# Layer 0's row steps behind its edge checks, constants and checks moved, later turns of the supports: one change to a four-layer graph kernel

## The chip, the cores and the metric

The kernel runs on one NeuronCore of a Trainium2 chip. The time is the device time of one execution in microseconds (us); lower is better. PE is the matrix engine, DVE the vector engine, ACT the scalar engine, POOL is GpSimd, and SP is the engine whose queue issues the large loads.

## The reference, cut to what matters

4096 nodes with 64 features each pass through four layers over the same dense 4096 x 4096 adjacency matrix of zeros and ones. Each layer ends with `x = layernorm(x + layer(x, adj))`.

```python
# layer 0: mean over the neighbours
deg = clip(sum(adj, axis=1) + 1.0, 1.0)
h   = (adj @ X + X) / deg
out = relu(concat([X, h]) @ W + b);  out = out / max(norm(out), 1e-12)
# layers 1 and 3: hyperbolic attention
adj_att   = sigmoid(left[:, None] + right[None, :] + b_att) * adj
x_local   = logmap(x[:, None, :], x[None, :, :])        # a vector for each pair of nodes
support_t = einsum('ij,ijd->id', adj_att, x_local);  out = proj(expmap(x, support_t))
# layer 2: at most 100 last neighbours, weighted by powers of 0.5
support = x @ weight
rank = cumsum(adj != 0, axis=1);  out = (mask * 0.5**(k - pos)) @ support + bias
```

## The kernel before, in words

**Tiling.** The nodes are 32 blocks of 128 rows (`NB = 32`, `P = 128`). The targets are taken in four groups of 1024 columns, in the order `GROUPS` = s 3, 2, 1, 0. For each group a layer walks `g` from 15 down to 0; each step loads two blocks of sources against the group's 1024 targets, a tile `edges` of 128 x 2 x 1024 numbers, 1 MB (`load`, line 708, on SP's queue). The matrix doesn't stay on the chip: each of the four layers reads its 64 tiles again. The pool of these tiles has 6 buffers, so load n+6 is issued when every reader of load n is done, and SP issues strictly in order.

**The check.** The fast path holds only where all edges are 0 or 1, so each of the 64 tiles is checked once in the whole kernel, by one DVE instruction over the tile (`check`, line 871). `checked_later(s, g)` names the tiles that are checked not in layer 0 but in layer 2 (`load_2`): g in 0, 1, 2, 3, 5, 7, 9, 11, half of each group. So in layer 0 a tile has two readers, the eight matmuls of line 1571 and, for g = 15, 14, 13, 12, 10, 8, 6, 4, the check.

**Row work and its turns.** What is done to a group's rows once their sums are there (in layer 0 `end_0`, then `norm_rows` and `prepare`, which make the operands of layer 1) is written as generators. `later` puts a generator in a queue, `tick` runs one step of each queue whose time has come, and `yield n` says how many ticks the next step waits. Layer 0 calls `tick(4)` after each load's matmuls, layer 2 `tick(1)` after each block. PE and ACT keep the order in which the program is written down (`manual_schedule(engines=FIXED)`); the instructions of DVE are put in order by a scheduler, so a row step may stand before or behind a check. `mark` records the last instruction of the main work on each engine (in `pairs_last`), and where `anchored[0]` is true, gives each row instruction of PE, ACT or DVE an order behind it. In layer 0 `anchored[0]` is false; from the second group of layers 1 and 3 on it is true.

**Layer 0 (line 1571).** Each load feeds eight matmuls of 512 columns. In the first group the loads are also interleaved with four pieces of x, split into bf16 parts by `parts_of` (lines 1472 to 1476). After the load g = 13 of the first group `constants()` (lines 1480 to 1494) is written down as one piece: a matmul that spreads the small vectors over the partitions (line 1481), its copy `given_b` (line 1482), eight small matmuls with the attention weights (line 855), and some fifty DVE instructions on one or two columns (`curved`, `att_columns`). Then follows `linear` for the group's own part (lines 1379 to 1390 and 1505). When a group's sums are complete, ACT copies them (lines 1596, 1604) and `end_0` is queued; its steps run during the next group. Its DVE chain goes from `deg` (1525) over `z` (1527 to 1548), `n_m`, `n_v` (924 to 938), `x`, `cx`, `y` (944 to 968) to `ys` (987) and `tt` (1006); PE then turns `ys` (1025).

**Layer 2.** The first pass (`wide_pass`) takes the groups 3 and 2 together, two loads a step; `narrow_pass` takes the others. Lines 1756 (running counts), 1763 (powers on ACT) and 1768 (weighted sums) are its work. In its early steps it also makes the last two blocks' `supports`: ACT rounds x to f16 (`x_hl`, 1403), GpSimd subtracts (1404), PE turns the two (1409) after a `yield 2`, ACT copies `x_t` (1412), PE multiplies (1419), ACT and DVE write `halves` (1425, 1426).

Of the kernel before, what the change touches and what calls it, by code (L numbers as in the profile page):

```python
# [21 lines left out]
D = 64  # L22
# [39 lines left out]
def gnn_stack_kernel(  # L62
# [509 lines left out]
    def stream(fits):  # L572

        with ExitStack() as st:
# [57 lines left out]
            def later(steps, second=False, wait=0):  # L632
                queues[int(second)].append([steps, place[1] + wait])

            def in_turn(tag, *parts):
                for part in parts:
                    yield from (part or ())
                done.add(tag)
# [5 lines left out]
            def need(tag):  # L644
                while tag not in done:
                    assert any(queues), tag
                    tick(1)
# [38 lines left out]
            def spare_ends():  # L686
                while held:
                    tick(1)
                spare.clear()
# [21 lines left out]

            def checked_later(s, g):

                return g in (0, 1, 2, 3, 5, 7, 9, 11)

            def grp(name, bufs=None):
                kw = {"bufs": bufs} if bufs else {}
# [129 lines left out]
                nc.scalar.dma_start(t, src[:, :, None, :].to_broadcast([1, 2, 2, D]))  # L847
                return t

            def att_columns(rows_of, name):  # L850


                t = aux.tile([P, 2], F32, name="aux")
                for u in range(2):
                    nc.tensor.matmul(
                        t[:, u : u + 1], rows_of[:, u].rearrange("p k d -> p (k d)"),
                        one_row[:, :1], start=True, stop=True,
                    )
                w = row.tile([P, 2], F32, name="att_w")
                V.tensor_copy(w, t)  # L860
                parts = keep.tile([P, 7], BF16, name=name)
                for k in range(3):
                    of = parts[:, k : k + 4 : 3]
                    V.tensor_copy(of, w)
                    V.tensor_sub(w, w, of)
                V.memset(parts[:, 6:], 1.0)
                return parts
# [530 lines left out]
            def supports(s):  # L1398


                xg = x_of(2)[:, blocks(s), :]
                hl = row.tile([P, WB, 2 * D], F16, name="x_hl")
                nc.scalar.copy(hl[:, :, :D], xg)
                nc.gpsimd.tensor_sub(hl[:, :, D:], xg, hl[:, :, :D])
                yield 2
                yield from free()
                t = take(F16, P, WW)
                for k in range(WB):
                    nc.tensor.transpose(t[:, k * P : (k + 1) * P], hl[:, k, :], ident16)
                yield near()  # L1410
                xt = row.tile([P, W], F32, name="x_t").bitcast(F16)
                nc.scalar.copy(xt, t)
                held.pop()
                yield near()
                yield from free()
                t = take(F32, P, WB, D)
                for k in range(WB):
                    for part in range(2):
                        nc.tensor.matmul(
                            t[:, k, :], xt[:, k * P : (k + 1) * P], w2_hl[:, part],  # L1420
                            start=part == 0, stop=part == 1,
                        )
                yield near()
                at = blocks(s)
                nc.scalar.copy(halves[:, at, :D], t)
                V.tensor_sub(halves[:, at, D:], t, halves[:, at, :D])
                held.pop()
                yield 1
# [25 lines left out]
            with ExitStack() as lp:  # L1454
# [23 lines left out]
                def constants():  # L1478

                    t = aux.tile([P, 2 * D + 3], F32, name="aux")  # L1480
                    nc.tensor.matmul(t, one_row, given, start=True, stop=True)
                    V.tensor_copy(given_b, t)
                    V.tensor_mul(c1, r_sb, r_sb)
                    V.reciprocal(c1, c1)
                    V.memset(c3, 1.0)
                    V.tensor_copy(ident16, ident)
                    V.memset(sum_w[:, D:], 0.0)
                    V.tensor_copy(sum_w[D:, :D], w0_sb[D:, :])
                    V.memset(count_w, 0.0)
                    V.memset(count_w[D:, D:], 1.0)  # L1490
                    V.tensor_copy(count_w[:D, :D], sum_w[:D, :D])
                    return (
                        curved(c1, "k1", 1e-15**0.5), curved(c3, "k3", 1e-15),
                        att_columns(att_rows1, "att1"), att_columns(att_rows3, "att3"),
                    )

                V.memset(third[:, :, D : D + 1], 1.0)
                parts_of(GROUPS[0])
# [8 lines left out]
                def end_0(s, tops):  # L1507
# [44 lines left out]
                        1, s, att1, batt1_sb, curve1, 1e-15, good[:, 0], 70  # L1552
                    )

                with tc.manual_schedule(engines=FIXED):
                    for s in GROUPS:
                        sums = [ps.tile([P, W], F32, name="acc") for _ in range(2)]
                        counts = [ps.tile([P, W], F32, name="acc") for _ in range(2)]
                        parts = ((first, sums, P), (third, counts, D + 1))
                        for g in reversed(range(NB // 2)):  # L1560
                            a, edge = load(s, g)
                            if s == GROUPS[0] and 2 * g % WB == WB - 2 and g > WB // 2:
                                parts_of(2 * g // WB - 1)
                            if not checked_later(s, g):
                                check(s, g, a, own.tile([P, 2, WW], BF16, name="junk"))
                            for k in (1, 0):
                                j = 2 * g + k
                                for lhs, accs, m in parts:
                                    for h in range(2):
                                        at = k * WW + h * W  # L1570
                                        nc.tensor.matmul(  # L1571
                                            accs[h][:m], lhs[:, j, :], edge[:, at : at + W],
                                            start=j == BLOCKS[0], stop=j == BLOCKS[-1],
                                        )
                            if g == s * WB // 2 + 1:

                                for lhs, accs, m in parts:
                                    for h in range(2):
                                        for k in range(SB):
                                            nc.tensor.matmul(  # L1580
                                                accs[h][:m, k * P : (k + 1) * P],
                                                lhs[:, s * WB + h * SB + k, :], ident_b,
                                                start=False, stop=False,
                                            )
                            if s == GROUPS[0] and g == NB // 2 - 3:
                                curve1, curve3, att1, att3 = constants()
                                nc.scalar.dma_start(w2_sb, w2)
                                nc.scalar.dma_start(w2_twice[:D], w2)
                                nc.scalar.dma_start(w2_twice[D:], w2)
                                later(in_turn((0, s), linear(0, s, w0_sb[:D, :], own_part)))  # L1590
                            tick(4)
                        need((0, s))
                        tops = []
                        for h in range(2):
                            top = row.tile([P, W], F32, name="sums", bufs=2)
                            nc.scalar.copy(top, sums[h])
                            low = (
                                row.tile([P, WB, D + 1], F32, name="u_1").rearrange(
                                    "p k f -> p (k f)"
                                )[: D + 1, :W]  # L1600
                                if h
                                else grp("w_att").rearrange("p k f -> p (k f)")[: D + 1]
                            )
                            nc.scalar.copy(low, counts[h][: D + 1])
                            tops.append((top, low))
                        later(end_0(s, tops))
                        if s == GROUPS[-1]:
                            need((0, s, "rows"))
                        if s > 0:
                            own_of = linear(0, s - 1, w0_sb[:D, :], own_part)  # L1610
                            later(in_turn((0, s - 1), own_of))

                spare_ends()


            place[0] = 1
# [286 lines left out]
```

## Time and profile before

| what | value |
|---|---|
| runs | 1061.79, 1062.61, 1067.7 us, median 1062.61 us |
| the profiled execution | 1063.81 us, of which its span, first to last instruction, is 1062.1 us |
| granted PE clock, mean | 0.975 of full |
| loads | 256 of 1 MB, four times 64 |

The stages, read from where the lines start and end:

| layer | from, to (us) |
|---|---|
| 0, groups 3, 2, 1, 0 (ACT starts to copy the sums) | 0, 54.2, 96.3, 139.7, 182.1 |
| 1 | 183 to 510 |
| 2, wide pass, then the narrow passes | 510 to 612, 612 to 720 |
| 3 and the end | 720 to 1062 |

How to read the profile: a row of the timeline has start and length in us, the engine, the line, the operation with its tiles, how many were merged, and in brackets how long the engine had been idle and what let it go. A row of the windows gives, for a stretch, its length, each engine's busy time with the number of instructions, the granted PE clock, the busy share of the DMA engines and what they moved in GB/s. A row of the waits gives in total how long an engine, or with a "q" its queue, waited for a group, how often, and the longest.

### The profile page before, as it was taken

To read this page: it belongs to the slowest core of one execution; us is meant where nothing else is said; L and a number is where in the kernel's file an instruction comes from. 1 tells how busy PE (TensorE), PEld (TensorE's weight loads), DVE (VectorE), ACT (ScalarE), POOL (GpSimd) and SP (SyncE) were. 2 spreads that over 40 slices of the span, in tenths; PEclk is the share of its full clock that TensorE was granted. 3 is DMA by queue.
4 is the path that set the end of the run, shared out by engine and by line. 5 is a ranking of instruction groups with operands and counts; after the bars stand their busy time and mean duration, and the time that the engine had idled before them with its cause. 6 is when DMAs were issued, how large, how long until landed. Compare 5 with 4: busy or idle time off the path is not lost.

```text
span 1062.1 us, 13509 instructions
## 1 busy us (share of the span) xinstructions
PE 981.6 (92%) x4760; PEld 401.9 (38%) x4845; DVE 900.2 (85%) x1383; ACT 753.1 (71%) x876; POOL 339.0 (32%) x695
## 2 busy tenths in 40 slices
PE   5998998889999999999999999999899999999991
PEld 2454554333333333333333344543333333333330
DVE  7577877788999999999475579858899999999996
ACT  0013122779989888898667688897898888888870
POOL 0011212480155365365210020104401562573660
PEclk8899999899999999999999999999999999999996
DMA  9999999755665666567589999996465765665600
GB/s 357 359 418 368 394 390 387 300 180 176 238 208 207 220 238 207 189 238 238 204 300 336 371 366 304 327 333 233 143 218 194 243 232 204 242 207 203 234 1 23
DMA packets 38580, 271.62 MB, mean 256 GB/s; under 512 B 4710, under 2 KB 4710, under 8 KB 5734
## 3 DMA queue, kind: packets, MB, share of 16 engines
q1 hardware_dynamic: 37728, 270.03, 69.6%
q8 instruction: 40, 0.66, 0.2%
q10 hardware_dynamic: 774, 0.63, 0.2%
q14 instruction: 38, 0.31, 0.1%
HBM read 269.58 MB, written 1.05 MB: 255 GB/s over the span
## 4 chain that ended last, share of the span: by engine, by line
PE 62%; DVE 21%; ACT 6%; POOL 6%; issue 2%; DMA 2%; ACTq 0%; SPq 0%; POOLq 0%; DVEq 0%
PE acc L1130 16%; PE z L1756 11%; PE z L1155 7%; PE z L1158 7%; PE z L1152 7%; DVE t L1179 6%; DVE t L1176 6%; PE acc L1571 5%; PE z L1768 3%; DVE junk L871 2%; PE z L1722 2%; DMA edges<-in_adj_dram 2%; ACT sq L1173 2%; ACT sq L1763 1%; POOL sq L1535 1%
## 5 line engine op out<-in xcount | busy, mean ns | idle before, releaser
L1176 DVE SCALAR_TENSOR_TENSOR t<-z,sig 128x1024 f32<-128x1024 f32 x256 | 309.1, 1219 | 22.4 <-ACT sq L1173 20.1
L1173 ACT ACTIVATE sq<-z 128x1024 f32<-128x1024 f32 x256 | 255.1, 1022 | 59.1 <-PE z L1158 29.2
L1179 DVE SCALAR_TENSOR_TENSOR t<-sq,t 128x2048 f32<-128x2048 f32 x127 | 293.3, 2309 | 0.3
L1170 ACT ACTIVATE sig<-left_b,right 128x1024 f32<-128x1024 f32 x256 | 286.6, 1149 | 3.6 <-DVE t L1176 3.2
L1130 PE MATMUL acc<-t,xe 128*64 128x512 f32 x1024 | 259.8, 611 | 7.9 <-DVE t L1179 7.0
L1155 PE MATMUL z<-lo_hi,hi_lo 128*128 128x512 f16 x512 | 194.4, 380 | 3.8 <-issue 1.1
L1158 PE MATMUL z<-dst,src 74*128 74x512 f16 x512 | 195.4, 382 | 0.0
L1152 PE MATMUL z<-edges,two_i 128*128 128x512 bf16 x463 | 181.8, 393 | 5.8 <-DVE t L1176 5.8
L1763 ACT ACTIVATE sq<-z 128x512 bf16<-128x512 f32 (+1 forms) x192 | 137.9, 741 | 43.0 <-PE z L1756 41.2
L1130 PEld LDWEIGHTS acc<-t,xe 128*64 128x64 f32 x1024 | 64.2, 137 | 137.2 <-issue 109.8
L871 DVE SCALAR_TENSOR_TENSOR t<-edges 128x2048 bf16<-128x2048 f32 x32 | 73.3, 2300 | 28.7 <-DMA edges<-in_adj_dram 28.5
L1152 PEld LDWEIGHTS <-two_i 128*128 128x128 bf16 x512 | 50.3, 98 | 124.7 <-issue 74.3
L1571 PE MATMUL acc<-edges,first 128*128 128x512 bf16 x241 | 77.9, 400 | 16.8 <-DMA edges<-in_adj_dram 16.3
L1756 PE MATMUL z<-edges,pass_by 128*128 128x512 bf16 x241 | 85.2, 390 | 6.8 <-ACT sq L1763 5.8
L1756 PE MATMUL z<-edges,enter 128*128 128x512 bf16 x248 | 86.3, 388 | 0.4
L871 DVE SCALAR_TENSOR_TENSOR junk<-edges 128x2048 bf16<-128x2048 f32 x32 | 73.1, 2284 | 15.7 <-DMA edges<-in_adj_dram 15.7
L1571 PE MATMUL acc<-edges,third 128*65 128x512 bf16 x256 | 81.1, 398 | 0.8 <-issue 0.2
L1158 PEld LDWEIGHTS <-src 74*128 74x128 f16 x512 | 49.3, 96 | 73.0 <-issue 11.6
L1155 PEld LDWEIGHTS <-hi_lo 128*128 128x128 f16 x512 | 50.4, 98 | 58.3 <-issue 12.8
L1279 POOL TENSOR_TENSOR w_att<-x,u 128x512 f32<-128x512 f32 x6 | 18.1, 3022 | 163.5 <-ACT u L1273 163.5
L1722 PE MATMUL z<-sq,halves 128*128 128x512 bf16 x122 | 45.9, 377 | 0.8 <-ACT sq L1763 0.6
L1535 POOL TENSOR_TENSOR sq<-z 128x512 f32<-128x512 f32 x4 | 10.1, 2524 | 114.2 <-DVE z L1533 94.6
(466 smaller groups left out, 1002.3 us busy)
## 6 DMA issues: line engine op xcount, KB each, us to landing
edges<-in_adj_dram SPq DMA_DIRECT2D x256, 1024.0 KB, 4.9
x<-in_x_dram SPq DMA_DIRECT2D x4, 256.0 KB
out_dram<-x ACTq DMA_DIRECT2D x2, 256.0 KB
out_dram<-x SPq DMA_DIRECT2D x2, 256.0 KB
w_sb<-in_L_gnn_W_dram ACTq DMA_DIRECT2D x1, 32.0 KB, 5.3
w_twice<-in_L_gnn_weight_dram ACTq DMA_DIRECT2D x2, 16.0 KB, 4.6
given<-in_L_gnn_b_dram ACTq DMA_DIRECT2D x1, 0.2 KB
given<-in_L_gnn_bias_dram ACTq DMA_DIRECT2D x1, 0.2 KB
```

The lines of the kernel that those rows point to most:

```text
L871: V.scalar_tensor_tensor(junk, a, 0.0, a, ALU.not_equal, ALU.not_equal, accum_out=odd[:, n : n + 1])
L1130: it = nc.tensor.matmul(acc[h * D : (h + 1) * D, :], xe[:, j, :], t[:, k, h * W : (h + 1) * W], start=j == BLOCKS[0], stop=j == BLOCKS[-1],)
L1152: nc.tensor.matmul(half, two_i, edge[:, at : at + W], start=True, stop=False)
L1155: nc.tensor.matmul(half, hi_lo[:, of], lo_hi[:, to], start=False, stop=False)
L1158: last = nc.tensor.matmul(half, src[:, of], dst[:, to], start=False, stop=True)
L1170: nc.scalar.activation(sig, left_b, AF.Sigmoid, bias=right[:, j : j + 1])
L1173: nc.scalar.activation(sq[:, k], zp, AF.Square, bias=ROOT + OFF, scale=-1.0 / UNIT)
L1176: V.scalar_tensor_tensor(ts[k][:, k], zp, 0.0, sig, ALU.max, ALU.mult)
L1179: V.scalar_tensor_tensor(t, sq, HIGH**2, t, ALU.add, ALU.mult)
L1571: nc.tensor.matmul(accs[h][:m], lhs[:, j, :], edge[:, at : at + W], start=j == BLOCKS[0], stop=j == BLOCKS[-1],)
L1756: nc.tensor.matmul(z[:, h : h + W], lhs, rhs[:, h : h + W], start=j == BLOCKS[0], stop=True, skip_group_check=True,)
L1763: weighed[0] = nc.scalar.activation(w, z[:, :n], AF.Exp, bias=-(OFF_EDGE + CUT) * LN2, scale=-LN2)
```

## The change

Four things are changed.

1. `anchored[0]` is true in layer 0 for all groups but the first, so the row steps of DVE written down there stand behind the last check written down before them.
2. `constants()` becomes a generator in the queue: one load between the spreading matmul and its copy, two loads before the first attention products, two before their columns, and so on; `linear` of the first group follows it. `att_columns` is split into its matmuls (`att_products`) and the rest.
3. `checked_later` also names g = 4 and 6 of groups 3 and 2: four checks leave layer 0 and are made in layer 2's wide pass.
4. `supports` waits 4 ticks instead of 2 in layer 2 between GpSimd's subtraction and PE's turn.

```diff
             def checked_later(s, g):
-                return g in (0, 1, 2, 3, 5, 7, 9, 11)
+                return g in (0, 1, 2, 3, 5, 7, 9, 11) or (s in GROUPS[:2] and g in (4, 6))
...
-            def att_columns(rows_of, name):
+            def att_products(rows_of):
...
+                return t
+
+            def att_columns(t, name):
...
                 nc.gpsimd.tensor_sub(hl[:, :, D:], xg, hl[:, :, :D])
-                yield 2
+                yield 4 if place[0] == 2 else 2
                 yield from free()
...
                     nc.tensor.matmul(t, one_row, given, start=True, stop=True)
+                    yield 4
                     V.tensor_copy(given_b, t)
+                    yield 8
                     V.tensor_mul(c1, r_sb, r_sb)
...
-                    return (
-                        curved(c1, "k1", 1e-15**0.5), curved(c3, "k3", 1e-15),
-                        att_columns(att_rows1, "att1"), att_columns(att_rows3, "att3"),
-                    )
+                    made.append(curved(c1, "k1", 1e-15**0.5))
+                    made.append(curved(c3, "k3", 1e-15))
+                    for rows_of, name in ((att_rows1, "att1"), (att_rows3, "att3")):
+                        w = att_products(rows_of)
+                        yield 8
+                        made.append(att_columns(w, name))
+                    yield 4
...
+                made = []
                 with tc.manual_schedule(engines=FIXED):
                     for s in GROUPS:
+                        anchored[0] = s != GROUPS[0]
...
                             if s == GROUPS[0] and g == NB // 2 - 3:
-                                curve1, curve3, att1, att3 = constants()
...
-                                later(in_turn((0, s), linear(0, s, w0_sb[:D, :], own_part)))
+                                own_of = linear(0, s, w0_sb[:D, :], own_part)
+                                later(in_turn((0, s), constants(), own_of))
                             tick(4)
                         need((0, s))
+                        curve1, curve3, att1, att3 = made
...
                 spare_ends()
+                anchored[0] = False
```

What the order of the built programs shows: POOL and SP have the same instructions in the same order. On PE only the constants' matmuls and the first group's `linear` (both spread over later loads) and the two turns of `x_hl` in layer 2 (each two blocks later) move. On ACT only the copies that follow these turns move. On DVE layer 0 is reordered; further on only the four added checks and one `halves` stand elsewhere.

In layer 0's groups 1 and 0 the order of DVE was `y`, `hl`, `xe`, check of g = 6, `ys`, the rest up to `tt`, check of g = 4, and before `y` stood also `xw` and six small steps; now it is `y`, check of g = 6, check of g = 4, then `hl`, `ys`, `xw`, `xe` and the rest. The check of g = 8 keeps its place in the middle of the reciprocal root of `n_m`.

## The prediction

> **What bounds the kernel now.** I read the windows by stage first, then the waits of SP's queue and of PE, then the timelines of the places that these named. The windows are layer 0's first group to its fourth, and a stretch in which nothing holds the loads back:
>
> ```profile
> 0.00:54.00 54.00, 41.02 (x172) 21.08 (x176) 34.47 (x114) 2.44 (x3) 1.22 (x13) 0.87 0.93 359
> 54.00:97.00 43.00, 38.92 (x221) 21.81 (x224) 33.84 (x86) 7.62 (x13) 8.82 (x9) 1.00 0.97 387
> 97.00:140.00 43.00, 38.85 (x235) 22.43 (x237) 34.56 (x98) 10.14 (x17) 8.74 (x9) 1.00 0.96 386
> 140.00:183.00 43.00, 39.94 (x247) 22.76 (x249) 35.94 (x102) 9.91 (x19) 8.69 (x9) 1.00 0.98 399
> 45.00:75.00 30.00, 29.80 (x170) 17.31 (x172) 17.57 (x32) 3.19 (x6) 3.01 (x1) 1.00 1.01 422
> ```
>
> Undisturbed, the loads run at 422 GB/s, 2.48 us for 1 MB (1.049e6 bytes); over layer 0 they get 359 to 399. PE is busy for 39 of 43 us in a group, so it is the next bound, close behind. Who holds the loads back (all of layer 0, then its last three groups) and what PE waits for:
>
> ```profile
> SPq L708 <- DVE junk L871: 103.6, 28, 6.3
> SPq L708 <- PE acc L1571: 37.7, 27, 7.5
> ...
> SPq L708 <- DVE junk L871: 97.3, 24, 6.3
> SPq L708 <- PE acc L1571: 10.5, 14, 1.4
> ```
> ```profile
> PE acc L1571 <- DMA edges<-in_adj_dram: 16.3, 13, 7.5
> PE aux L855 <- DVE given_b L1482: 4.3, 1, 4.3
> PE aux L1379 <- DVE z L1527: 1.5, 1, 1.5
> ```
>
> In the last three groups the queue waits for the checks, that is for buffers. The timeline of DVE in the third group shows why a check is late: the check of g = 6 stands behind `y` and `xe`, that of g = 4 behind twenty more row steps, and SP's next loads go out as they end, at 133.44 and 138.10.
>
> ```profile
> 129.80 0.69 DVE L968 TENSOR_TENSOR y<-x,ym 128x512 f32<-128x512 f32 x1
> ...
> 131.08 2.29 DVE L871 SCALAR_TENSOR_TENSOR junk<-edges 128x2048 bf16<-128x2048 f32 x1
> ...
> 135.74 2.28 DVE L871 SCALAR_TENSOR_TENSOR junk<-edges 128x2048 bf16<-128x2048 f32 x1
> ```
> ```profile
> 133.44 0.80 SPq L708 DMA_DIRECT2D edges<-in_adj_dram  x2
> ```
>
> The first group is another case: PE stands from 16.7 to 21.0 for `given_b`, which DVE makes behind its checks, and then runs at half clock until 33; until 82 it has no idle gap over 0.25 us, it is catching up.
>
> ```profile
> 21.04 1.01 PE L855 MATMUL aux<-one_row,xw 1*128 1x1 f32 x4 [4.33 <-DVE given_b L1482]
> ...
> 19.30:33.00 13.70, 10.93 (x34) 6.59 (x36) 11.67 (x60) 0.58 (x1) 0.00 (x0) 0.50 0.96 382
> ```
>
> Layer 2's wide pass is bound by PE (11.9 of 12 us in most slices), and its one hole is at the turn of `x_hl`. The row puts it down to DVE, but `un` is not read there: GpSimd's subtraction ended at 543.70, 60 ns before.
>
> ```profile
> 543.76 0.62 PE L1409 MATMUL aux<-ident,x_hl 128*128 128x128 f16 x8 [2.14 <-DVE un L756]
> ...
> 540.42 3.28 POOL L1404 TENSOR_TENSOR x_hl<-x,x_hl 128x512 f16<-128x512 f32 x1 [30.22 <-ACT x_hl L1403]
> 568.36 1.16 POOL L1404 TENSOR_TENSOR x_hl<-x,x_hl 128x512 f16<-128x512 f32 x1 [24.66 <-ACT x_hl L1403]
> ```
>
> [...] half clock after the gaps of 4.3 us (for 13.7 us) and of 2.14 us (for 3.4 us, from 545.0), none after 1.72 us at 89. [...] Here the subtraction took 3.28 us while a check began at 540.40, and 1.16 us at 568, where the check was the one drawn out (2.74 for 2.29 us).
>
> **The change, part by part.** The sum is made against the profiled execution, 1063.8 us (span 1062.1), which is 1.2 above the median of the runs.
>
> *Constants.* PE no longer stops at 16.7: it goes on with g = 12, and `given_b` is ready at 21 as now. The 4.3 us of waiting, 0.8 of smaller waits and half of the 8.3 us at half clock up to 33 (4.1), in which it was working, fall away. PE then comes up to the loads. By 10 us 2.6 MB are in; the first group's 16 loads and x are 17.8 MB, so the last lands at 10 + 15.2/0.421 = 46, plus some 1.3 [...] (in all four groups the last landed 1.0 to 1.7 after its bytes' turn), and PE ends 1.9 later: 49.2, where the copies start at 54.2 now. One new wait is inside: the second pair of attention products needs the buffer that DVE frees behind the check of g = 10 (ends at about 29), PE would be there at 27.4; 2 us, perhaps a half clock again, which the loads in the buffers mostly cover: 49.5. First group: -4.7.
>
> *Checks first, and four fewer.* Load n+6 waits for check n: the check of g = 8 lets the load of g = 2 out, that of g = 6 the load of g = 0, that of g = 4 the second load of the next group. Second group: with 6 and 4 gone only g = 8 is left, whose check ended 28.7 us after the first group's sums (82.9 - 54.2). At 49.5 + 28.7 = 78.2 its load goes out, while the loads before it have landed at 10 + 28.8/0.421 = 78.4; a load alone needs 4.9 us to land, 2.4 more than its bytes: a hole of about 2 us. Third group: g = 8 comes 2 us earlier, because `f` no longer stands ahead of it waiting for ACT's logarithm (1.61 us idle at 106.05). `y` comes 1.1 us earlier still (without `xw` 0.55 and small steps 0.5), so g = 6 ends 33.7 after the sums and not 37.1, and g = 4 directly behind it, 36.0 and not 41.7. The loads before that of g = 0 take until 10 + 47.7/0.421 + 2 = 125.3, or 35.3 after sums at 90, so with the 2.4 us of latency under 1 us of hole is left. Fourth group: g = 6 at 33.2 after the sums and not 35.6. The three groups then take the bytes' time, 16.8 MB / 0.421 = 39.9 us each, with PE's 39 just below: 40.5 on average, where they took 42.1, 43.4 and 42.4. Sum -6.4. The last group's end comes to 49.5 + 121.5 = 171.0 for 182.1.
>
> What it costs: the checks come at their landings, and row steps queue behind them, `hl` and `ys` behind two (4.6 us). In the fourth group `ys` is then ready 36.2 us after the sums and PE turns it at 38.4; GpSimd's pieces by 38.4, needed at 40.5; so nothing. `tt` comes at 40.2, and behind it ACT's logarithms delay the copies that end the layer by about 0.9: +0.9. Bounds: 0 if these slip into ACT's idle time, +3 if PE stands in each of the last two groups. Layer 1's first blocks come from groups that are long done; its start shifts with the sums.
>
> *Four more checks in layer 2.* 4 x 2.29 = 9.2 us of DVE in the wide pass, where it is busy 55 of 102 us. From g = 7 on a step checks two tiles, 4.6 us, in PE's 5.8 us; buffers stay PE's to free. 0; if that cover failed at most the 4.6 us of one step.
>
> *Supports.* Two blocks later is 5.8 us on PE: the subtraction ends at 543.7 as now, PE comes at 547.4. The 2.14 us go, and the half clock after it: the rows of line 1768 start at 539.55, 545.37 and 550.12; two blocks of 2.89 us behind 539.55, with 0.9 for the turn and product, make 546.3. So 3.8 us. Next is the PE product behind it, three us later, whose results DVE writes at 552, used at 561: no wait. Bounds: -2.1 (clock falls anyway) to -3.8.
>
> Sum: -4.7 - 6.4 + 0.9 - 3.8 = -14.0; 1063.8 - 14.0 = 1049.8 in the profiled execution's terms, 1048.6 on the median. I say **1048.6**.
>
> **The rivals.** *A, the forecast*, 66%: 1044 to 1053.5. The low end is layer 0 at the bytes' rate without holes (three groups of 39.9, 1.8 us less; the first 1.5 less; no 0.9); the high end is supports at 2.1 and half of the 6.4.
> *B, the DVE chain sets the pace*, 15%: g = 8 keeps its place in the chain, and if its ends stay where they are the later loads are as late; the second sum falls from 6.4 to about 1: 1048.6 + 5.4 = 1054. For it: DVE is busy 36 of 43 us. Against: the two checks that let out the last loads do move.
> *C, the supports' gain is eaten* by a later wait for `halves` or the added checks, 10%: 1048.6 + 3.8 = 1052.4.
> *D, the change does nothing*, 4%: PE catches up in the second group anyway, layer 0 ends as now: 1062. Against it, the loads run below their rate in every group.
> *E, slower*, 5%: in the third and fourth group PE reaches the turn of `ys` before DVE has it. If it stands there for over 2 us, the clock goes to half as at 19.3, 13.7 us costing 6.8; with the two checks' 4.6 that is 11.4 for each group, 22.8 for both, against gains of 4.7 + 1.6 + 3.8 in the first two groups and the wide pass: 1062.6 + 12.7 = 1075. It decides where `ys` comes over 4 us later in its group than I put it; the 2.2 us between 36.2 and 38.4 speak against it.
>
> **How the numbers follow.** A's middle is the forecast. The range holds A, C and B's middle: 1044 to 1055; left out are D, E, half of B and A's edges, some 18%. This kernel's measurement tells about 0.5% (5.3 us) from no change. Faster by more: A, B, C, 91%; within: D and a bit of B, 5%; slower: E, 4%.
>
> **What would show it.** Right: no half clock from 19.3 to 33 and no wait for `given_b`; ACT's first copies at about 49; SP's wait for checks in the last three groups well below 97 us; DMA share 0.99 and more; layer 0's end at 170 to 172; no idle before `x_hl`'s turn and no half clock behind it. Wrong: groups that still take 42 us or more, a PE wait at line 1025, or a wide pass still of 102 us.

## The result, and the profile after

| | before | after |
|---|---|---|
| median of 5 runs each (us) | 1063.37 | 1053.52 |
| lowest to highest | 1061.79 to 1067.7 | 1051.73 to 1055.81 |
| the profiled execution, and its span | 1063.81, 1062.1 | 1051.74, 1050.0 |

The ratio is 0.9895, with a 95% interval of 0.9863 to 0.9927: about 1% faster. The forecast was 1048.6 with a range of 1044 to 1055, so the direction and the range hold, and the change gave 9.9 us where 14.0 were worked out.

The windows of the changed kernel, layer 0's four groups from ACT's copies to the next copies, and then a stretch of the wide pass, with the columns as before (length, PE, PEld, DVE, ACT, POOL, clock, DMA share, GB/s):

```profile
0.00:51.60 51.60, 41.31 (x176) 19.77 (x177) 31.30 (x111) 2.44 (x3) 1.22 (x13) 0.90 0.97 388
51.60:92.00 40.40, 37.93 (x218) 21.24 (x216) 29.09 (x75) 6.88 (x12) 6.75 (x9) 1.00 0.98 396
92.00:133.00 41.00, 39.69 (x241) 22.70 (x240) 36.11 (x98) 10.43 (x17) 4.52 (x9) 1.00 1.00 408
133.00:174.80 41.80, 40.06 (x249) 22.73 (x248) 36.94 (x109) 9.07 (x17) 6.43 (x9) 1.00 1.00 413
520.00:540.00 20.00, 20.00 (x121) 7.97 (x120) 16.55 (x47) 14.99 (x19) 3.17 (x1) 1.00 0.93 352
```

The groups are 2.6, 1.7, 2.4 and 0.6 us shorter, and the loads move more in each. In the wide pass PE is busy for all of the 20 us in which the turn of `x_hl` falls. The waits of SP's queue (the last three groups) and of PE (all of layer 0):

```profile
SPq L708 <- DVE junk L874: 77.6, 22, 5.9
SPq L708 <- PE acc L1581: 22.3, 16, 2.6
```
```profile
PE acc L1581 <- DMA edges<-in_adj_dram: 15.3, 9, 7.3
```

SP's wait for checks fell from 97.3 to 77.6 us; its wait for PE grew from 10.5 to 22.3. PE waits for nothing but loads: neither `given_b` nor `ys` nor `z` is in its list. The third group on DVE, and SP's issue. Times in a group are counted from ACT's copies that end the group before it, whose rows DVE works on here; so `y` starts at 31.3 us (123.28), where it started at 33.5 before:

```profile
123.28 0.69 DVE L971 TENSOR_TENSOR y<-x,ym 128x512 f32<-128x512 f32 x1
123.89 2.29 DVE L874 SCALAR_TENSOR_TENSOR junk<-edges 128x2048 bf16<-128x2048 f32 x1
126.22 2.29 DVE L874 SCALAR_TENSOR_TENSOR junk<-edges 128x2048 bf16<-128x2048 f32 x1
```
```profile
126.25 7.77 SPq L708 DMA_DIRECT2D edges<-in_adj_dram  x7
```

The two checks stand directly behind `y`, with nothing between them. They end at 34.2 and 36.5 us (37.1 and 41.8 before), and the load of g = 0 goes out at the end of the first. From there the group's end adds up: the load lands 5.4 us after its issue and ACT's copies start 1.4 us later, 41.0 in all; before it was 37.1, 4.9 and 1.4, that is 43.4. So in the third group the DVE chain and the check behind it still set the end, only earlier (PE comes free from its turn of `ys` just as the load lands, at 131.6).

The first group has a stop of PE left, for the load of g = 10, and a half clock that begins in it, at 22.7; in the wide pass the subtraction takes what it took and PE isn't waiting any more:

```profile
23.58 1.01 PE L1581 MATMUL acc<-edges,first 128*128 128x512 bf16 x2 [3.02 <-DMA edges<-in_adj_dram]
```
```profile
22.70:32.90 10.20, 9.32 (x24) 3.94 (x24) 9.24 (x40) 0.00 (x0) 0.00 (x0) 0.50 1.02 422
```
```profile
533.05 3.17 POOL L1407 TENSOR_TENSOR x_hl<-x,x_hl 128x512 f16<-128x512 f32 x1 [30.21 <-ACT x_hl L1406]
```

So the stop of 4.3 us for `given_b` became one of 3.0 us for a load. Between 22.7 and 32.9 PE is at half clock, yet the loads run at 422 GB/s: they don't falter under it as they did before (382).

Between the two profiled executions, span against span: layer 0 -7.2 (182.1 to 174.8), the wide pass -3.9 (96.4 to 92.5), layer 3's first group -1.6 (95.7 to 94.1) and its last +1.0, everything else under 0.3 each; together -12.1. In layer 3 only the place of the half clock differs (two stretches of 3.4 us near 726 and 763 before, none there after, one at 1022.8), so the 0.6 that its two groups give together is not the change's.

### The profile page after: what moved, and what is told of

It reads as the page before. It is cut to its first block, busy times and chain, and to the rows that moved or that the text cites. A ratio compares the mean times of both kernels' runs of the same rounds, so it can differ in the third digit from the quotient of the medians.

```text
span 1050.0 us, 13594 instructions
## 1 busy us (share of the span) xinstructions
PE 984.8 (94%) x4845; PEld 399.6 (38%) x4845; DVE 903.4 (86%) x1383; ACT 752.7 (72%) x876; POOL 335.3 (32%) x695
## 4 chain that ended last, share of the span: by engine, by line
PE 62%; DVE 19%; POOL 7%; ACT 6%; DMA 4%; issue 2%; SPq 0%; POOLq 0%; ACTq 0%; DVEq 0%
PE acc L1133 16%; PE z L1768 11%; PE z L1155 8%; PE z L1161 7%; PE z L1158 7%; DVE t L1182 6%; DVE t L1179 5%; PE acc L1581 5%; DMA edges<-in_adj_dram 3%; PE z L1780 3%; DVE junk L874 3%; PE z L1734 2%; ACT sq L1176 2%; ACT sq L1775 1%; ACT sig L1173 1%
## 5 line engine op out<-in xcount | busy, mean ns | idle before, releaser
L1155 PE MATMUL z<-edges,two_i 128*128 128x512 bf16 x512 | 200.9, 392 | 5.4 <-DVE t L1179 5.3
L1775 ACT ACTIVATE sq<-z 128x512 bf16<-128x512 f32 (+1 forms) x192 | 138.0, 741 | 39.1 <-PE z L1768 38.4
L874 DVE SCALAR_TENSOR_TENSOR t<-edges 128x2048 bf16<-128x2048 f32 x36 | 82.2, 2299 | 19.9 <-DMA edges<-in_adj_dram 19.7
L1581 PE MATMUL acc<-edges,first 128*128 128x512 bf16 x256 | 81.9, 402 | 15.8 <-DMA edges<-in_adj_dram 15.3
L874 DVE SCALAR_TENSOR_TENSOR junk<-edges 128x2048 bf16<-128x2048 f32 x28 | 64.0, 2284 | 9.4 <-DMA edges<-in_adj_dram 9.3
L1734 PE MATMUL z<-sq,halves 128*128 128x512 bf16 x128 | 48.1, 377 | 0.6 <-ACT sq L1775 0.6
L1387 ACT COPY x_t<-aux 64x512 f32<-64x512 f32 x8 | 4.6, 577 | 57.4 <-PE aux L1382 57.4
```

The lines of the kernel that those rows point to most:

```text
L874: V.scalar_tensor_tensor(junk, a, 0.0, a, ALU.not_equal, ALU.not_equal, accum_out=odd[:, n : n + 1])
L1155: nc.tensor.matmul(half, two_i, edge[:, at : at + W], start=True, stop=False)
L1581: nc.tensor.matmul(accs[h][:m], lhs[:, j, :], edge[:, at : at + W], start=j == BLOCKS[0], stop=j == BLOCKS[-1],)
L1775: weighed[0] = nc.scalar.activation(w, z[:, :n], AF.Exp, bias=-(OFF_EDGE + CUT) * LN2, scale=-LN2)
```

## The experiments

The theory was the forecast's: three places are bound by three different waits, and each part of the change shortens one. Its rivals for what remained of layer 0: the delay of PE, slowed by half clock in the first group, is carried on; the checks still hold the loads; or the loads' own rate, and how late a load lands behind its bytes, set the end.

All profiles in one table. The columns are the lengths in us of layer 0's groups, layer 0's end, the wide pass, and layer 3's first segment, each from the starts of ACT's copies (layer 3's from DVE's copy of layer 2's last sums). Each row but the last column comes from one profile:

| kernel | group 1 | 2 | 3 | 4 | end | wide | layer 3 | median, runs |
|---|---|---|---|---|---|---|---|---|
| before | 54.2 | 42.1 | 43.4 | 42.4 | 182.1 | 96.4 | 95.7 | 1063.4 |
| after | 51.6 | 40.3 | 41.0 | 41.8 | 174.8 | 92.5 | 94.1 | 1053.5 |
| after, again | 53.1 | 40.4 | 40.9 | 41.8 | 176.2 | 92.5 | 95.6 | 1055.5, one |
| supports after 2 | 52.9 | 40.8 | 40.9 | 42.4 | 177.0 | 95.1 | 95.7 | 1056.3 |
| no order in layer 0 | 50.4 | 41.4 | 43.4 | 42.0 | 177.2 | 92.5 | 96.9 | 1056.6 |
| constants whole | 54.7 | 40.4 | 41.1 | 42.6 | 178.8 | 92.5 | 96.8 | 1056.9 |
| four checks back | 52.5 | 40.3 | 42.5 | 41.9 | 177.2 | 92.5 | 95.7 | 1054.9 |
| matmuls added | 50.7 | 40.3 | 42.5 | 41.8 | 175.3 | 92.5 | 95.5 | 1053.1 |
| no checks in layer 0 | 52.3 | 39.1 | 40.2 | 40.6 | 172.2 | 92.5 | 95.6 | 1050.5, one |
| fewer count matmuls | 51.4 | 41.4 | 43.3 | 43.0 | 179.1 | 92.5 | 94.1 | 1058.1, one |
| both left out | 51.8 | 40.7 | 39.8 | 40.7 | 173.0 | 92.5 | 95.7 | 1051.1, one |
| check of g = 8 moved too | 51.4 | 40.1 | 41.0 | 41.8 | 174.3 | 101.6 | 95.7 | 1064.1 |
| 4 buffers | 53.5 | 45.8 | 45.8 | 45.8 | 190.9 | 101.1 | 95.7 | 1077.4, one |
| last group's checks moved | 51.8 | 40.6 | 41.3 | 41.2 | 174.9 | 92.5 | 95.5 | 1053.6 |

The last column has medians of different rounds, in which the kernel before lay between 1061.7 and 1065.1 us. Whole times are therefore compared by their ratios to it, and the intervals of these are about 3 us to each side: of the kernels run several times, only the one with the check of g = 8 moved is clearly apart from the changed kernel by its whole time. What is said of the parts rests on the stages of the profiles.

**Supports after two blocks again.**

```diff
-                yield 4 if place[0] == 2 else 2
+                yield 2
```

> The changed kernel with one part undone: supports wait 2 ticks again. Theory (PE stall plus half clock): the wide pass, from the end of layer 1 to the first copies of its sums, goes from 92.5 back to 96.4 us, PE is idle about 2.1 us before the turn of x_hl and its clock falls to half for 3.4 us behind it; the whole is 3.9 us slower than the changed kernel, about 1057.4. Rival (the gain came from elsewhere in the pass, or the clock falls anyway): 92.5 to 94.7, total at most 2.1 slower.

Median 1056.32 us, ratio 0.992 (0.9893 to 0.9947). The wide pass takes 95.06 us, 2.5 more than the changed kernel. The turn, in PE's timeline:

```profile
538.29 0.62 PE L1412 MATMUL aux<-ident,x_hl 128*128 128x128 f16 x8 [2.00 <-DVE un L756]
```

The wait of 2 us is back, without a half clock behind it this time (the granted clock is 1.00 from 522.4 to 542.4), so the pass lies between the two expectations (96.4, and at most 94.7). The part is worth 2.5 us where the clock stays up, and 3.9 where, as in the profile of before, it falls.

**No order behind the checks in layer 0.**

```diff
-                        anchored[0] = s != GROUPS[0]
+                        anchored[0] = False
```

> The changed kernel with anchored false in all of layer 0. Theory (the check of g = 6, behind y and xe, lets the last load of a group out late): first and second group as in the changed kernel within 0.5 us; in the third and fourth the check of g = 6 ends 36 to 37 us after the sums instead of 34, and they take 42.5 and 42.3 us instead of 41.0 and 41.8; layer 0's end 1.5 to 2.5 us later. Rival (these groups are at the rate of the loads or of PE already, so the order of DVE is worth nothing): layer 0's end within 0.5 us of 174.8.

Median 1056.57 us, ratio 0.9927 (0.9899 to 0.9955). The third group takes 43.4 us, just as before the change, the second 41.4; PE waits at one row step:

```profile
102.19 0.60 PE L1382 MATMUL aux<-ident,x 128*64 128x128 f32 x4 [1.54 <-DVE z L1535]
```

And DVE in the third group, which begins at 91.7:

```profile
126.58 2.29 DVE L874 SCALAR_TENSOR_TENSOR junk<-edges 128x2048 bf16<-128x2048 f32 x1
131.24 2.28 DVE L874 SCALAR_TENSOR_TENSOR junk<-edges 128x2048 bf16<-128x2048 f32 x1
```

The two checks end at 37.1 and 41.8 us in the group, to the tenth as before the change; in every profile with the order, where both are made and PE's work is whole, they end between 34.2 and 34.6, and 36.5 and 36.9. The order is what moves the checks, and with them the third group's end. The three groups take 126.8 us, 3.6 more than in the changed kernel (123.2), but 1.3 of that only makes up for a first group that ended earlier; layer 0's end is 2.3 later.

**Constants in one piece.**

```diff
-                                later(in_turn((0, s), constants(), own_of))
+                                for _ in constants():
+                                    pass
+                                later(in_turn((0, s), own_of))
```

> The changed kernel with the constants in one piece again, behind g = 13 of the first group. Theory (the stop of PE for given_b and the half clock behind it are made up only in part later): first group ends at 53.5 to 54.2 us instead of 51.6, and of these 2 to 2.6 us at least half is still there at the end of layer 0 (175.8 to 177). Rival (later groups catch up, since the loads set their pace): layer 0 ends within 0.5 us of 174.8.

Median 1056.9 us, ratio 0.9919 (0.989 to 0.9948). PE's stop is back, and the loads falter behind it, at 314 GB/s (the changed kernel: 419 in the same stretch):

```profile
23.90 0.85 PE L854 MATMUL aux<-one_row,xw 1*128 1x1 f32 x4 [4.00 <-DVE given_b L1486]
```
```profile
30.00:40.00 10.00, 9.93 (x51) 5.39 (x51) 6.62 (x21) 0.58 (x1) 0.00 (x0) 0.95 0.85 314
```

The first group is at 54.7 us. Five profiles have the changed kernel's first group (after, after again, supports after 2, no order in layer 0, last group's checks moved); they give 50.4 to 53.1, and the three of them whose loads began as slowly as here (6.09 to 6.19 MB in 20 us, here 6.22) 52.6 on the mean. The spreading is worth about 2 us.

**Four checks back in layer 0.**

```diff
-                return g in (0, 1, 2, 3, 5, 7, 9, 11) or (s in GROUPS[:2] and g in (4, 6))
+                return g in (0, 1, 2, 3, 5, 7, 9, 11)
```

> The changed kernel with the four checks of g = 6 and 4 of the first two groups back in layer 0. Theory (with the order behind the checks they are early enough): first group as it was within 0.5 us, second group 40.3 to 41.3 us, layer 0's end at most 1 us later; the wide pass 92.5 us as it was, with four checks fewer. Rival (the dropped checks are what let the loads out): second group 42 us, layer 0's end 1.7 us or more later. Rival on layer 2 (the added checks cost there): the wide pass gets shorter by over 0.5 us.

Median 1054.86 us, ratio 0.9909 (0.9877 to 0.9941). The wide pass takes the same 92.5 us, so the four checks cost nothing there. The second group, where two of them are again, takes the same 40.3 us. The third is 1.5 longer, but so it is in the next kernel, which leaves the four checks in layer 2. These lengths show no gain of this part in layer 0; layer 0's end leaves it open (see the repetition below).

**Twelve matmuls added** between g = 11 and the attention products; their results aren't used.

```diff
-                    yield 8
+                    yield 4
+                    warm = aux.tile([P, W], F32, name="aux")
+                    for _ in range(12):
+                        nc.tensor.matmul(
+                            warm, ident_b, first[:, NB - SB :, :], start=True, stop=True
+                        )
+                    yield 4
```

> The changed kernel with 12 more matmuls of 512 columns on data at hand (2.6 us of PE work, results unused) between the matmuls of g = 11 and the first attention products of the first group, where PE waits 3.0 us for the load of g = 10 and then runs at half clock for 10 us. Theory P (what was missing of layer 0's gain is PE's half clock in the first group, carried through the next groups): no half clock from 22 to 33 us, first group ends at 47 to 50 us, layer 0's end 2 to 4 us before 174.8 to 177.0. Theory L (from the second group on the loads' own rate, 396 to 413 GB/s with the DMA engines busy all the time, sets the pace): the first group ends earlier as well, but the second takes as much longer, and layer 0's end moves by under 1 us.

Median 1053.08 us, ratio 0.9889 (0.9862 to 0.9916). The clock in the first group is 1.00 throughout, and the group ends at 50.7, 0.9 earlier; but layer 0 ends at 175.3 and the time is the changed kernel's. So the theory that the half clock of the first group is carried through layer 0 falls. The stretch in which the changed kernel runs at half clock, here:

```profile
20.00:30.00 10.00, 9.39 (x44) 4.25 (x42) 9.47 (x49) 0.00 (x0) 0.00 (x0) 1.00 1.02 423
```

**No checks in layer 0, fewer count matmuls, and both.** The first leaves out layer 0's 28 checks, the second three quarters of the matmuls with `third`.

```diff
-                            if not checked_later(s, g):
+                            if False:
...
                                 for lhs, accs, m in parts:
+                                    if lhs is third and j % 8 not in (0, 7):
+                                        continue
```

> The changed kernel without any check in layer 0 (28 left out, those tiles are not checked at all; their flags are set to zero). Theory L (loads at their rate): second to fourth group 40 to 41.8 us as in the changed kernel, layer 0's end at most 2 us earlier. Theory C (the checks still hold the loads back): 39.5 us each and layer 0's end 3.5 us or more earlier. Theory P (PE behind): no more than a few tenths for the groups.

> The changed kernel with three quarters of layer 0's matmuls of the third part and the counts left out (so neighbour counts and the smallest part of the sums are wrong); PE's work per group falls from 38 to 40 us to about 28. Theory P: first group ends at 46 to 48 us, each later group 39.9 us or less at 421 GB/s, layer 0's end at 168 to 170. Theory L: the first group ends earlier, the others keep 40.5 to 41.8 us, layer 0's end 172 to 174. Theory C: same as L.

> Both: no checks in layer 0 and three quarters of the third part's matmuls left out. Then only the loads are left, and all theories agree that this shows their floor: 68.2 MB at 410 to 421 GB/s, layer 0's end between 166 and 172 us. If it is 172 the loads alone explain what was missing; if 167, PE and the checks do.

The windows of the kernel without checks, second to fourth group, and of the one without either, second group:

```profile
52.30:91.30 39.00, 37.66 (x213) 21.23 (x216) 16.59 (x70) 6.85 (x11) 4.78 (x9) 1.00 1.01 420
91.30:131.60 40.30, 39.18 (x239) 22.80 (x241) 17.82 (x82) 10.46 (x18) 4.26 (x9) 1.00 1.01 420
131.60:172.20 40.60, 38.78 (x237) 22.35 (x240) 18.39 (x86) 9.27 (x18) 5.10 (x9) 1.00 1.01 421
```
```profile
51.80:92.50 40.70, 32.92 (x166) 18.27 (x168) 16.61 (x70) 6.87 (x11) 4.87 (x9) 0.83 1.01 421
```

Without checks the loads run at 420 GB/s in every group from the second on, and layer 0 ends at 172.2. With less of PE's work alone it ends at 179.1, later than with all of it, which no theory had expected: PE is busy for 32 to 33 us of each of the last three groups and its granted clock there is 0.87 to 0.94 (38 to 40 us and 1.00 in the changed kernel), and the third group's last two checks end at 36.2 and 38.5 us in it, 2 later than in the changed kernel. With both left out it ends at 173.0, and the first group still at 51.8. So the end of layer 0 is the loads' at about 172 to 173 in these two executions; of what the changed kernel takes above that, 2 to 3 us are the checks that remain (groups 2 to 4 together 123.2 us with them, 119.9 and 121.2 without).

**The check of g = 8 moved too**, two more for the wide pass.

```diff
-(s in GROUPS[:2] and g in (4, 6))
+(s in GROUPS[:2] and g in (4, 6, 8))
```

> The changed kernel with the check of g = 8 of groups 3 and 2 made in layer 2's wide pass as well: two checks fewer in layer 0, two more behind PE's work later. If what is left of the checks holds layer 0's loads (the run without checks moved 420 GB/s in groups 2 to 4, this change 396 to 413), the second group is faster by about 0.5 to 1 us, the first by nothing, layer 0's end near 174, and the wide pass stays at 92.5 us because two tiles' checks still fit beside PE's 5.8 us: about 1052.5 to 1053. If the checks in the wide pass are not free any more, it takes over 94 us there and the time is 1054 to 1056. In the narrower theory that the rate of layer 0 varies by itself between executions, its end is anywhere from 173 to 177 and the time is 1053.5.

Median 1064.06 us, ratio 1.0025 (1.0001 to 1.0048): the whole gain is gone. The second group moves 420 GB/s, but is only 0.2 us shorter where 0.5 to 1 was expected; the wide pass takes 101.6 us, 9.1 more, a size that was not expected at all (and the narrow pass behind it 53.3 for 50.7). The stretch of it, and the three rows that say why, DVE, ACT and PE:

```profile
555.00:565.00 10.00, 2.79 (x16) 0.93 (x15) 9.83 (x17) 2.46 (x3) 0.74 (x1) 0.83 0.64 243
```
```profile
562.79 0.68 DVE L1372 TENSOR_TENSOR x<-z,y 128x512 f32<-128x512 f32 x1
563.56 0.62 ACT L1406 CAST x_hl<-x 128x512 f16<-128x512 f32 x1 [7.54 <-DVE x L1372]
565.16 1.01 PE L1768 MATMUL z<-edges,pass_by 128*128 128x512 bf16 x2 [7.36 <-ACT sq L1775]
```

And the same two steps in the changed kernel:

```profile
549.86 0.69 DVE L1372 TENSOR_TENSOR x<-z,y 128x512 f32<-128x512 f32 x1
556.62 0.61 ACT L1406 CAST x_hl<-x 128x512 f16<-128x512 f32 x1
```

PE's row names `sq`, ACT's powers, but ACT was standing: in its fixed order the cast of `x_hl` comes before those powers, and the cast waits for `x` on DVE. In the changed kernel `x` is done at 550.5 and the cast comes at 556.6, a margin of 6.1 us. Ahead of `x` DVE makes five checks there, and eleven here, though only two were added: g = 8 was the one step among g = 9 to 4 that had no checks, and the row chain ran through it (in the changed kernel there is no check between those that start at 537.2 and at 547.7). With a pair of checks in every step the scheduler puts about 1 us of row steps between two checks. Six checks of 2.28 us are 13.7; less the 6.1 of margin that is 7.6, the 7.5 that ACT stood. The rest of the 9.1 falls together with 6.8 us of half clock from 561.6 (the granted clock is 0.83 from 555 to 565 and 0.95 from there to 600). Nothing was run here to separate these two.

**Four buffers.**

```diff
-            loads = pool("f_loads", 6)
+            loads = pool("f_loads", 4)
```

> The changed kernel with 4 buffers for the loads and not 6: fewer loads in flight, load n+4 waits for the readers of load n. If the first group's last load lands late because loads that are in flight together share the engines, its landing is nearer to its bytes' turn (2.2 us behind it in the changed kernel, about 1.3 here), but each check now holds a load that is needed two loads sooner: the groups of layer 0 take 44 us and more, its end is past 182, and the time is past 1062. If two buffers in six are never needed, layer 0's end stays at 175 and the time at 1053.5.

One run, 1077.37 us. Every group from the second on takes 45.8 us, and the wide pass 101.1: four buffers are too few in both. The last load of the first group is issued at 43.8 and lands at 51.7, 1.1 us behind its bytes' turn (18.0 MB in, by the windows' sums), where the changed kernel, which issues it at 38.4 and lands it at 49.1, has 2.3. That fits the theory that loads in flight delay each other, which was an estimate; the rate differs too (370 GB/s from 20 to 30 us, for 423), so it isn't shown.

**The changed kernel once more.**

> The changed kernel once more, for the spread of one execution to the next: if the profile of it was an average one, layer 0's end is at 174 to 176 and the start of layer 3 (first group's segment) at 94 to 97 us depending on where half-clock stretches fall. The kernels with the same order in layer 0 gave 174.8 and 177.0.

One run, 1055.49 us, layer 0's end 1.4 us later. The first 20 us of it and of the first profile:

```profile
0.00:10.00 10.00, 2.74 (x7) 1.20 (x8) 5.79 (x25) 0.24 (x1) 1.22 (x13) 1.00 0.76 247
10.00:20.00 10.00, 8.18 (x39) 3.75 (x38) 6.91 (x20) 1.04 (x1) 0.00 (x0) 1.00 0.97 368
```
```profile
0.00:10.00 10.00, 2.72 (x7) 1.19 (x8) 5.52 (x23) 0.23 (x1) 1.22 (x13) 1.00 0.79 275
10.00:20.00 10.00, 10.00 (x51) 4.64 (x50) 9.97 (x23) 1.06 (x1) 0.00 (x0) 1.00 1.00 397
```

The repetition moved 0.57 MB less in its first 20 us (6.15 for 6.72), which at 421 GB/s is 1.35 us of the 1.47 by which its first group is longer. From 20 us on both move 419 to 423 GB/s. In layer 3 its first segment takes 95.6 us for 94.1. So the first profile of the changed kernel was a good one, and its median lies 1.8 us above it.

The start explains much of what is unlike in layer 0's ends. As an estimate, take from each end the time that the bytes missing from 6.72 MB need at 421 GB/s. Then the three profiles with the changed layer 0 (after, again, supports after 2) end at 174.8, 174.8 and 175.8 us; four checks back at 176.6 (6.49 MB), no order at 177.0 (6.67), constants whole at 177.6 (6.22), and the two kernels without checks at 170.8 and 171.7 (6.13 and 6.16). So each part brings layer 0 some 1 to 3 us, that of the four checks least surely: it is hardly more than the three alike differ by, from one profile.

**The last group's checks moved too.** Since the wide pass has no room left, g = 4 and 6 of the last group were left to the second narrow pass.

```diff
-(s in GROUPS[:2] and g in (4, 6))
+(s not in GROUPS[2:3] and g in (4, 6))
```

> The changed kernel with g = 4 and 6 of the last group (s = 0) left to layer 2 as well, so that its two checks are made in the second narrow pass. DVE is busy for 22.4 of 34 us in that pass's second half, so there is room: fourth group of layer 0 in 40.6 to 41.2 us and not 41.8 (the run without any check took 40.6), nothing elsewhere, 1052.5 to 1053. If a row step of that pass comes behind the two checks, as happened in the wide pass with two more checks, PE stands for ACT there and the second narrow segment takes over 55 us (53.8 in the changed kernel): 1055 and more. If ACT's logarithms and not the checks set the end of the fourth group, it stays at 41.8.

Median 1053.56 us, ratio 0.9913 (0.9885 to 0.9941). The fourth group takes 41.2 us for 41.8, the narrow pass the same 53.8. The 0.6 us is there in the profile and doesn't show in the time. No version that clearly beats the changed kernel was found.

## Why the prediction was right, and where it was not

**First group, -4.7: the mechanism right, the size not.** PE passes `given_b` and comes up to the loads, as forecast; the group ends at 51.6, not 49.5, and at 52.0 on the mean of the five profiles with this first group. The term that was mis-sized is the way from bytes to copies: "the last lands at 10 + 15.2/0.421 = 46, plus some 1.3 ... and PE ends 1.9 later". The profile has the bytes in at 46.8 (from 10 to 20 us the loads move 397 GB/s, not 421), the landing 2.3 later, and the copies 2.6 after that. Each was a bit too low. About 1 us of the 2.1 is the half clock, for which I had allowed 0.3: with nearly as quick a start of the loads, the kernel with added matmuls and the one without order had none and reached 50.7 and 50.4. No execution reached 49.5, not even with neither checks nor all of PE's work (51.8, but with 10.2 us of half clock and a start 1.3 us slower); whether the other 1 us can be had stays open. The early stretch of the loads, which I took from one profile, differs by as much between two executions of one program.

**Groups 2 to 4, -6.4, and +0.9 for ACT: right within a microsecond.** The forecast puts them at 121.5 + 0.9 = 122.4 us; the profile has 123.2, its repetition 123.1. The steps came as written: g = 6 was forecast to end 33.7 after the sums and ended 34.2 (36.0 and 36.5 for g = 4), in the fourth group 33.2 and 33.9; g = 8 in the second group 28.7 and 27.9. The third group's hole was 1.1 us in two stops of PE, forecast under 1. ACT's two logarithms and a copy do stand ahead of the last copies, but what the order costs there is more than the 0.9:

```profile
173.72 0.21 ACT L1039 ACTIVATE tt<-tt 128x8 f32<-128x8 f32 x1 [7.32 <-DVE q L1011]
173.84 0.19 ACT L1040 ACTIVATE q<-q 128x8 f32<-128x8 f32 x1
173.94 0.99 ACT L1032 COPY hi_lo<-aux 128x1024 f16<-128x1024 f16 x1
174.83 0.59 ACT L1607 COPY sums<-acc 128x512 f32<-128x512 f32 x1
```

The copies come 2.8 us after the last landing (172.0); 1.4 is what the second and third group take for this, and the fourth without the order. The 1.9 of the forecast is the first group's of before. About half of the other 1.4 is PE, which turns `ys` as the load lands and begins its matmuls 0.7 us after it; the rest is ACT. What is not shown is the split: the second group, which was to need the four moved checks, takes 40.3 us with them back, and whether they bring layer 0 anything stays open.

**Four more checks in layer 2, 0: right, but its bound wasn't.** The wide pass takes 92.5 us with them and without. "If that cover failed at most the 4.6 us of one step" is wrong: two checks more cost 9.1 us. I had counted checks against PE's time for a step, and not the row chain that shares DVE with them, nor ACT, which stands in its fixed order for the end of that chain. The four checks are free because g = 4 and 6 come after that chain's `x`; its margin is 6.0 us with them back in layer 0 (`x` done at 553.0, cast at 559.0) and 6.1 with them here.

**Supports, -3.8: right to 0.1 in the profile** (-3.9), of which 2.5 are the wait and the rest the half clock (3.4 us) that followed it in the profile of before and not in the experiment. I took the upper end; over many executions it should lie between.

**The sum.** -14.0 was to give 1049.8 us in the profiled execution's terms; that took 1051.74, with 1.0 of its 12.1 from layer 3 and other places where the change does nothing. On the median the miss is 4.9 us. By the profiles at hand some 2.5 of it lie in the first group (52.0 for 49.5), 1.0 in the next three (123.45 on the mean of the three profiles with this layer 0, for 122.4), and 0.8 comes from the profile of before, which lies 0.4 above the median of five runs, not 1.2; the rest is not accounted for. That the median fell into the range is in part the range's width: 1053.5 is the upper edge of the forecast's own case. And of its signs of being right four did not come: there was half clock from 22.7 to 32.9, the first copies came at 51.6 and not at about 49, the DMA share was 0.97 and 0.98 in the first two groups, and layer 0 ended at 174.8 and not at 170 to 172.

**The rivals.** That the DVE chain sets the pace (1054) gives nearly the measured time, but not by its mechanism: `y` and the checks moved as forecast, and the third group shrank by 2.4 us. What is true in it is that the third group's end still follows that chain (34.2, 5.4 and 1.4 us), and not the bytes. The supports' gain was not eaten. PE didn't stand for `ys`: no such wait is in its list. The wait behind the check of g = 10, which was to be 2 us, didn't come: DVE's copy freed the buffer at 28.2 and PE made its second pair of products at 34.0. The loads' stop of 3.0 us came in its place.

## What to carry to other kernels

Where loads bound a stage, put its end together from the bytes' time, the lag of the last landing and the work behind it, each from several executions, before counting what is removed from the engines: here a floor of 171 to 173 left some 10 us of layer 0's 182, and the change got 6 to 7 of them (two executions). Work that is moved under another engine's time has to fit in the gaps that a dependent chain on its own engine lives on, and not only in the sum of free time; find the step that waits for the end of that chain and read its margin (6.1 us here) first. And before a sum is read to a microsecond, run the same program twice.

## What the runs showed of the hardware

- The same stop of PE was followed by half clock in one profile and not in the other. In layer 3's first segment the stop of 1.31 us had half clock behind it before (3.4 us, from 725.9) and none after, and the stop of 2.9 us the same (3.4 us from 763.4, and none). In the wide pass half clock came behind a stop of 2.14 us (before, 3.4 us from 545.0) and not behind one of 2.00 us (supports after 2). So in these traces the length of a stop alone doesn't tell whether the clock falls; the "over 2 us" of the forecast's rival E was an estimate from stops of 2.14 us (half clock) and 1.72 us (none), and the stop of 1.31 us is against it. Nor was half clock always behind the stop, as the forecast has it: at the stop of 4.3 us of before, from 16.7 to 21.0, it began at 19.3, 2.6 us into it.
- In the traces of before and after, the half-clock stretches were of 3.4 us (at 186.5, 545.0, 725.9 and 763.4 before, at 179.7 and 1022.8 after), 6.8 (at 196.8 before, 189.9 after), 10.2 (at 22.7 after) and 13.7 us (at 19.3 before), that is, close to multiples of 3.4; the last one runs to the program's end, from 1043.3 before and from 1033.1 after. The 10.2 us in the changed kernel's first group, where the loads ran on at 422 GB/s, cost about 1 us there (51.6 us, and 50.7 without half clock, with the matmuls added) and nothing that could be seen at layer 0's end (174.8 and 175.3).
- With three quarters of one operand's matmuls left out, layer 0 became slower (179.1 us in one run, for 174.8 to 177.0 in three with all of them) and its clock lower (0.87 to 0.94 in groups 2 to 4, for 1.00).
- The loads' sustained rate was 419 to 423 GB/s in the undisturbed stretches shown here, but the first 20 us moved 6.15 or 6.72 MB in two executions of one program.
- In the wide pass of the kernel with the check of g = 8 moved, one check, from 565.61, took 3.24 us for 2.28; GpSimd's subtraction ran beside it until 566.69.
